# Attention and a quantised feed-forward: the maximum of h over partitions through TensorE, the first group's integers by chunks, gate and p integers further ahead, k_o alone ahead of the branch

## The chip, the cores and the metric

The kernel runs on one core of a Trainium2 chip. Its engines are TensorE (PE; its weight loads are shown as PEld), VectorE (DVE), ScalarE (ACT), GpSimd (POOL) and SyncE (SP, which here only issues DMA transfers). Each engine works through its own list of instructions in order, and semaphores hold an instruction until its inputs are there. The metric is the device time of one execution in microseconds (us). The kernel before takes 1007.1 us, the median of three runs (1004.01 to 1007.13).

## The reference

The input x has 2 x 2048 rows of 512 numbers; there is a context of 2 x 128 rows. Layernorm has no weights here. Cut to what matters:

```python
x = x + xattn(layernorm(x), ctx, Wq, Wkv)       # one head of 512, 128 keys
h = act_qdq(layernorm(x))                       # 16 bits, ONE scale for the whole tensor
up   = act_qdq(h @ dequant4(w_up).T)            # 1536 columns
gate = act_qdq(h @ dequant4(w_gate).T)          # 1536 columns
sig  = round(sigmoid(gate) * 65536) / 65536
p    = act_qdq(gate * sig)
o    = act_qdq(p * up)
out  = x + o @ dequant4(w_down).T
```

`act_qdq` takes the maximum of the absolute values over the whole tensor, divides it by 32767 for a scale, and rounds the tensor to whole multiples of that scale. So each of h, gate, p, up and o needs a maximum over everything before its first integer can be made. The weights are rounded to 4 bits in blocks of 32.

## The kernel before

The 4096 rows are worked in eight groups t of 512 (TG). The 1536 columns of gate and up are twelve chunks f of 128, taken four at a time (k = 0, 1, 2). In the projections the columns lie on the 128 partitions, the rows along the free axis. An integer of 16 bits is not multiplied as such: it is split into parts that TensorE multiplies exactly, a high part (`sa`, the integer over 4096, rounded), the rest, and a combined third part. The weights are split in three as well. One chunk of a projection for one group, called a row of work below, is `project`: eight matmuls into a sum q (four pieces c of the 512 inner numbers, two parts each) and four into a sum e. ScalarE evacuates q, VectorE subtracts e.

The kernel has four stages.

- **Front** (lines 257 to 506). For each group: x is loaded and transposed, scores, softmax (`e`), `turn` transposes the softmax weights (`pe`) and copies them to SBUF (`eT`), `attend` multiplies with the values (`po`) and adds x (`xt`), `normalise` makes h (Square with a sum, then a power -0.5 on GpSimd, then Identity), and `lift` transposes h into the large tile hT by way of PSUM. The work of neighbouring groups is interleaved. For the last group `attend` and `normalise` go tile by tile of 128 rows. `hmax` collects the maxima of h. In between, a generator prepares the weights of gate (`split_weights`, advanced in steps).
- **Gate** (lines 534 to 588). `over_partitions` reduces hmax along the free axis on VectorE and over the partitions on GpSimd; `act_scale` makes the scale s_h and its reciprocal r_h. hi[t] are the integers of group t, made out of hT: those of group 0 in four pieces on VectorE, those of the others alternately by VectorE and ScalarE, all of them ahead of the gate loop in the program. Then hT's space is given up, and the pools `wkb2` (two g4 buffers) and `wprep` take it. `split_integers` makes the parts. For each group and each k four rows of work give a g4 of 1 MB, which goes to DRAM (`gate_d`); `gmax` collects the maxima. The weights of up and down are prepared one step a row.
- **Up** (lines 597 to 788). Groups run from last to first. The work is counted in 24 tiles j of four chunks and 48 halves c of two chunks (c = 2j + h). A half is two rows of work, an evacuation (`u`, L726), a subtraction (L727), and a store to `up_d`. Beside it `next_gelu` turns a loaded gate tile into integers gi and sq with three ScalarE passes over 128 x 2048 (L624 to L626) and loads the tile after the next; there are two gate buffers and three pairs gi, sq. `integers_of_p` makes p (one VectorE product, L661) in one of three tiles `kept_p` and stores it to `p_d`. `bound` forms |u| times p and keeps its largest value per partition (`pumax`); `fetch_best` finds, per partition, the half where that was largest and fetches its u and p rows with two indirect transfers on GpSimd. The last two halves are still at hand. The exact maximum of the rounded products of these three (`most`) goes through a second all-reduce to `top`, and a flag tells whether that maximum is certain; if it is not, a slow general path recomputes it (a branch at L926, not taken in these runs).
- **Output** (lines 794 to 1024). o's integers and parts are made per 128 rows on VectorE and ScalarE, and each of the 32 sets of rows takes 24 matmuls into yq and 12 into ye with the weights wd. ScalarE scales yq by q_o, GpSimd adds x, VectorE adds ye times e_o, and the rows are stored.

The order of instructions on each engine is fixed when the kernel is built, by a planner that goes through the program by priority (earlier lines first) and by a cost model of when inputs are ready. `in_order` forces one instruction behind another on the same engine, without a wait. All loads and stores named above, other than the two first gate loads and the fetches (GpSimd) and one weight load (ScalarE), are issued by SP in one list, where an issue that must wait holds those behind it.

## Time and profile before

| what | us |
|---|---|
| median of three runs | 1007.1 |
| the profiled execution | 1005.54 |
| its span, first to last instruction | 1003.7 |
| PE busy in the span | 942.7 |
| DVE busy | 810.7 |
| ACT busy | 548.3 |
| POOL busy | 89.6 |
| last transposes of h end | 171.96 |
| first gate matmul | 177.02 |
| first up matmul | 455.62 |
| last up matmul ends | 719.95 |
| first output matmul | 734.52 |

Times in the profile count from the span's start. A timeline line gives the start, the duration, the engine, the line of the kernel, the operation, the tiles it writes and reads, and in brackets how long the engine was idle before it and whose work ended that. A row of work takes TensorE 2.72 us at the full granted clock (the q sums of neighbouring rows start at 379.64, 382.36 and 385.08). The granted clock is either full or half in this trace; it is half after an idle stretch, and after the restart at 734.52 it stays half until 739.9.

### The profile page before, as it was taken

To read this page: it belongs to the slowest core of one execution; us is meant where nothing else is said; L and a number is where in the kernel's file an instruction comes from. 1 tells how busy PE (TensorE), PEld (TensorE's weight loads), DVE (VectorE), ACT (ScalarE), POOL (GpSimd) and SP (SyncE) were. 2 spreads that over 40 slices of the span, in tenths; PEclk is the share of its full clock that TensorE was granted. 3 is DMA by queue.
4 is the path that set the end of the run, shared out by engine and by line. 5 is a ranking of instruction groups with operands and counts; after the bars stand their busy time and mean duration, and the time that the engine had idled before them with its cause. 6 is when DMAs were issued, how large, how long until landed. Compare 5 with 4: busy or idle time off the path is not lost. (4 is left out here: it accounts for less than half of the span.)

```text
span 1003.7 us, 11683 instructions
## 1 busy us (share of the span) xinstructions
PE 942.7 (94%) x4321; PEld 762.9 (76%) x4321; DVE 810.7 (81%) x1000; ACT 548.3 (55%) x652; POOL 89.6 (9%) x67
## 2 busy tenths in 40 slices
PE   6997884999999999999999999999779999999998
PEld 5765652788888878887788788888557888888886
DVE  4579874999998989645899789887889999888882
ACT  2277786532333223226998998897454445444331
POOL 0101111000000000000000000000011232222221
PEclk9999896999999999999999999999879999999999
DMA  9177652987886666698899798988885676755611
GB/s 345 32 304 283 220 220 79 401 313 303 330 355 248 265 210 210 224 353 328 306 363 375 258 366 328 378 320 328 288 311 215 206 269 222 250 190 160 245 66 43
DMA packets 103596, 263.72 MB, mean 263 GB/s; under 512 B 6064, under 2 KB 46000, under 8 KB 94832
## 3 DMA queue, kind: packets, MB, share of 16 engines
q1 hardware_dynamic: 102496, 259.02, 69.4%
q0 software_dynamic: 512, 2.88, 0.8%
q10 hardware_dynamic: 528, 1.05, 0.3%
q8 instruction: 34, 0.56, 0.2%
q14 instruction: 26, 0.21, 0.1%
HBM read 136.05 MB, written 126.88 MB: 262 GB/s over the span
## 5 line engine op out<-in xcount | busy, mean ns | idle before, releaser
L528 PE MATMUL q_g<-parts_g,wg 128*128 128x512 f32 x768 | 195.0, 394 | 5.1 <-ACT parts_g L236 5.1
L528 PEld LDWEIGHTS q_g<-parts_g,wg 128*128 128x128 f32 x768 | 143.5, 189 | 35.4 <-ACT parts_g L236 5.8
L579 ACT ACTIVATE g<-q_g 128x512 f32<-128x512 f32 x96 | 57.3, 599 | 169.6 <-PE q_g L528 158.9
L528 PE MATMUL q_u<-parts_u,wu 128*128 128x512 f32 x576 | 142.4, 390 | 0.6 <-ACT u L726 0.6
L528 PEld LDWEIGHTS q_u<-parts_u,wu 128*128 128x128 f32 x576 | 108.1, 188 | 23.3 <-ACT u L726 1.0
L874 PE MATMUL yq<-wd,o_parts 128*128 128x512 f32 x512 | 122.1, 391 | 0.0
L874 PEld LDWEIGHTS yq<-wd,o_parts 128*128 128x128 f32 x512 | 96.9, 189 | 20.3
L532 PE MATMUL e_g<-parts_g,wg 128*128 128x512 f32 x384 | 104.0, 392 | 0.1
L580 DVE CUSTOM_DVE_ANT_0 g<-g,e_g 128x512 f32<-128x512 f32 x96 | 64.4, 681 | 37.2 <-PE e_g L532 37.0
L532 PEld LDWEIGHTS e_g<-parts_g,wg 128*128 128x128 f32 x384 | 72.3, 189 | 15.6 <-DVE parts_g L238 0.5
L889 POOL TENSOR_TENSOR qx<-yqs,x 128x512 f32<-128x512 f32 x32 | 63.7, 1991 | 204.3 <-ACT yqs L887 167.9
L874 PE MATMUL yq<-first_wd,o_parts 128*128 128x512 f32 x256 | 65.5, 399 | 13.2 <-ACT o_parts L863 13.2
L887 ACT ACTIVATE yqs<-yq,q_o 128x512 f32<-128x512 f32 x32 | 22.0, 686 | 101.8 <-PE yq L874 101.8
L532 PE MATMUL e_u<-parts_u,wu 128*128 128x512 f32 x288 | 77.1, 390 | 0.0
L866 DVE SCALAR_TENSOR_TENSOR o_parts<-sa,oi 128x1536 fp32r<-128x1536 int16 (+2 forms) x41 | 62.8, 1548 | 15.6 <-PE ye L882 15.6
L863 ACT CAST o_parts<-sa 128x1536 fp32r<-128x1536 int16 (+2 forms) x41 | 48.6, 1189 | 43.9 <-DVE sa L860 43.9
L670 DVE CUSTOM_DVE_ANT_0 ua<-ua,pi 128x1024 f32<-128x1024 f32 x46 | 55.9, 1220 | 16.9 <-ACT ua L669 16.7
L862 DVE SCALAR_TENSOR_TENSOR o_parts<-sa,oi 128x1536 fp32r<-128x1536 int16 (+2 forms) x41 | 59.5, 1451 | 10.9 <-PE yq L874 8.5
L874 PEld LDWEIGHTS yq<-first_wd,o_parts 128*128 128x128 f32 x256 | 48.9, 192 | 24.4 <-ACT o_parts L863 14.2
L727 DVE TENSOR_TENSOR u<-u,e_u 128x1024 f32<-128x1024 f32 x47 | 56.9, 1216 | 12.0 <-ACT u L726 11.9
L661 DVE SCALAR_TENSOR_TENSOR pi<-gi,k_p,sq 128x2048 int16<-128x2048 int16 x24 | 56.4, 2349 | 9.7 <-ACT sq L626 9.7
L882 PE MATMUL ye<-wd,o_parts 128*128 128x512 f32 x256 | 63.2, 389 | 0.0
(185 smaller groups left out, 1553.7 us busy)
## 6 DMA issues: line engine op xcount, KB each, us to landing
gate_d<-g SPq DMA_DIRECT2D x24, 1024.0 KB, 5.5
up_d<-u SPq DMA_DIRECT2D x48, 512.0 KB, 7.2
gt<-gate_d SPq DMA_DIRECT2D x22, 1024.0 KB, 8.6
u<-up_d SPq DMA_DIRECT2D x21, 1024.0 KB, 6.5
parts_d<-parts_g SPq DMA_DIRECT2D x6, 3072.0 KB, 10.9
parts_u<-parts_d SPq DMA_DIRECT2D x6, 3072.0 KB, 13.4
p_d<-pi SPq DMA_DIRECT2D x24, 512.0 KB, 9.7
p<-p_d SPq DMA_DIRECT2D x84, 128.0 KB, 3.3
```

Source lines behind the costliest of these rows:

```text
L528: nc.tensor.matmul(q, lhsT=w[:, s, c, :], rhs=parts[:, s, c, :], start=(c + s == 0), stop=(c + s == ND))
L532: nc.tensor.matmul(e, lhsT=w[:, 2, c, :], rhs=parts[:, 2, c, :], start=(c == 0), stop=(c == ND - 1))
L579: nc.scalar.activation(g4[:, i, :], q, AF.Copy, scale=1.0 + 1.0 / BASE)
L580: nc.vector.tensor_tensor_reduce(g4[:, i, :], g4[:, i, :], e, 1.0, LOWEST, ALU.subtract, ALU.max, gtop[:, m : m + 1])
L661: nc.vector.scalar_tensor_tensor(pi, gi, k_p, sq, ALU.mult, ALU.mult)
L670: nc.vector.tensor_tensor_reduce(ua, ua, pi, 1.0, 0.0, ALU.mult, ALU.max, pumax[:, c : c + 1])
L727: less = nc.vector.tensor_tensor(u4[:, both, :], u4[:, both, :], e, ALU.subtract)
L862: made.append(nc.vector.scalar_tensor_tensor(parts[1][:, c], sa[:, c], -BASE, oi[:, c], ALU.mult, ALU.add))
L866: return nc.vector.scalar_tensor_tensor(parts[2][:, c], sa[:, c], BASE + 1.0, oi[:, c], ALU.mult, ALU.subtract)
L874: nc.tensor.matmul(q, lhsT=parts[s][:, f, :], rhs=wd[f][:, s, :], start=(f + s == 0), stop=(f + s == NF))
L882: nc.tensor.matmul(e, lhsT=parts[2][:, f, :], rhs=wd[f][:, 2, :], start=(f == 0), stop=(f == NF - 1))
L889: nc.gpsimd.tensor_tensor(qx, qs, x1[:, m % NU, :], ALU.add)
```

## The change

Four things are changed.

1. `over_partitions_by_pe` is a helper made out of what the kernel did for u: a reduction on VectorE, a transpose on TensorE that lays the 128 partial maxima along every partition's free axis, and a reduction of that. It now serves h too, in a PSUM tile of the front's pool, before the front's pools close. The reduction over partitions on GpSimd remains for gate, for `top` and in the branch. In the front, the last group's eT is copied by VectorE.
2. `first_integers` makes group 0's integers and parts by chunks: chunk 0 rounded by VectorE, 1 to 3 by ScalarE, with the casts between them; the third parts come after all others. In the first tile (n = 0) the q sums of the first two chunks come ahead of their e sums. The integers of groups 1 to 7 stand behind the evacuations and subtractions of the first four rows. The two g4 buffers are two pools; the first lies outside hT's space, which is given up after the first tile. The preparation of up's weights begins at n = 1, with two steps a row for that tile.
3. In the up stage `next_gelu` has two more extra places, after halves 19 and 31 (before: after 1 and 13), and `next_p` has two, at halves 17 and 27. The p of a tile stands behind the evacuation of its first half, no longer ahead of the tile. The load of wd chunks 4 to 7 stands ahead of the store of half 43, no longer behind it.
4. `scale_of_o` is cut in two. `factor_of_o` (k_o) stays ahead of the branch; s_o, q_o and e_o are made after it, behind the first set of output rows. The branch now copies its maximum to a_o.

```diff
         return [a[:, i : i + 1] for i in range(len(stats))]
+    def over_partitions_by_pe(pool, tag, shape, stats, name):
+        m = const.tile([P, 1], F32, name=f"m_{name}")
+        nc.vector.tensor_reduce(m, stats, AX.X, ALU.max)
+        rows = pool.tile(shape, F32, tag=tag, name=f"rows_{name}")
+        rows = rows[:, 0, :P] if len(shape) == 3 else rows[:, :P]
+        nc.tensor.transpose(rows, m.to_broadcast([P, P]), ident)
+        a = const.tile([P, 1], F32, name=f"a_{name}")
+        nc.vector.tensor_reduce(a, rows, AX.X, ALU.max)
+        return a
...
                 eT = wk2.tile([P, NJ, P], F32, tag="eT", name=f"eT_{g}")
-                nc.scalar.copy(eT, pe)
+                if g < NG - 1:
+                    nc.scalar.copy(eT, pe)
+                else:
+                    nc.vector.tensor_copy(eT, pe)
                 return eT
...
             lift(NG - 1, hs.pop(NG - 1))
+            a_h = over_partitions_by_pe(ps_o, "o", [P, D], hmax, "h")
...
+            project_q(w, parts, q)
+            project_e(w, parts, e)
+        def project_q(w, parts, q):
             for c in range(ND):
...
                     )
+        def project_e(w, parts, e):
             for c in range(ND):
...
+        def first_integers(pool_a, r_h):
+            n = hi[0]
+            a = pool_a.tile([P, ND, TG], I16, tag="sa", name="sa_g0")
+            parts = homes[0].tile([P, 3, ND, TG], F32R, tag="parts", name="parts_g0")
+            rounded, casts, made = [], [], []
+            for c in range(ND):
+                if c == 0:
+                    made.append(nc.vector.tensor_scalar(n[:, c], hT[:, c, :TG], r_h, QMAX, ALU.mult, ALU.min))
+                else:
+                    rounded.append(nc.scalar.activation(n[:, c], hT[:, c, :TG], AF.Copy, scale=r_h))
+                made.append(nc.vector.tensor_scalar(a[:, c], n[:, c], 1.0 / BASE, None, ALU.mult))
+                casts.append(nc.scalar.copy(parts[:, 0, c], a[:, c]))
+                made.append(
+                    nc.vector.scalar_tensor_tensor(parts[:, 1, c], a[:, c], -BASE, n[:, c], ALU.mult, ALU.add)
+                )
+                if c:
+                    in_order(rounded[c - 1], casts[c - 1])
+            for c in range(ND):
+                made.append(
+                    nc.vector.scalar_tensor_tensor(
+                        parts[:, 2, c], a[:, c], BASE + 1.0, n[:, c], ALU.mult, ALU.subtract
+                    )
+                )
+            in_order(*made)
+            return parts, casts[-1]
+        def integers_of_h(t):
+            if t % 2:
+                return nc.vector.tensor_scalar(hi[t], hT[:, :, ts(t, TG)], r_h, QMAX, ALU.mult, ALU.min)
+            return nc.scalar.activation(hi[t], hT[:, :, ts(t, TG)], AF.Copy, scale=r_h)
         with ExitStack() as c2:
             wg = [load_parts(wg_d, f, "wg") for f in range(NF)]
-            s_h, r_h = act_scale(*over_partitions(hmax, name="h"), "h")
+            s_h, r_h = act_scale(a_h, "h")
...
             wk1 = c2.enter_context(tc.tile_pool(name="wkb1", bufs=1))
-            for c in range(ND):
-                nc.vector.tensor_scalar(hi[0][:, c], hT[:, c, :TG], r_h, QMAX, ALU.mult, ALU.min)
-            first = split_integers(wk1, homes[0], hi[0], [ND, TG], "g0", ND)
+            first, last_cast = first_integers(wk1, r_h)
             table = const.tile([P, 1], F32, name="table")
-            nc.scalar.activation(table, unit, AF.Sigmoid)
-            for t in range(1, NG):
-                if t % 2:
-                    nc.vector.tensor_scalar(hi[t], hT[:, :, ts(t, TG)], r_h, QMAX, ALU.mult, ALU.min)
-                else:
-                    nc.scalar.activation(hi[t], hT[:, :, ts(t, TG)], AF.Copy, scale=r_h)
-            hpool.__exit__(None, None, None)
-            home1 = tc.tile_pool(name="parts1", bufs=1, side="right")
-            homes.append(ctx.enter_context(home1))
-            wk2 = c2.enter_context(tc.tile_pool(name="wkb2", bufs=2))
-            wpp = c2.enter_context(tc.tile_pool(name="wprep", bufs=1))
+            in_order(last_cast, nc.scalar.activation(table, unit, AF.Sigmoid))
+            g4_homes = [c2.enter_context(tc.tile_pool(name="g4_0", bufs=1))]
             ps_m = c2.enter_context(tc.tile_pool(name="ps_m", bufs=3, space=PSUM))
...
-            steps = chain(split_rows(wpp, ps_t, w_up, wu_d, "u"), split_down(wpp, ps_t))
-            groups, wu = {}, []
+            steps, groups, wu = None, {}, []
             for t in range(NG):
...
                     n = t * NK + k
-                    g4 = wk2.tile([P, NQ, TG], F32, tag="g4", name=f"g4_{n}")
+                    g4 = g4_homes[n % 2].tile([P, NQ, TG], F32, tag="g4", name=f"g4_{n}")
+                    sums = [
+                        [ps_m.tile([P, TG], F32, tag=tag, name=f"{tag}_g{NQ * n + i}") for tag in "qe"]
+                        for i in range(2)
+                    ]
+                    if n == 0:
+                        for i in range(2):
+                            project_q(wg[i], parts, sums[i][0])
                     for i in range(NQ):
                         m = NQ * n + i
-                        q = ps_m.tile([P, TG], F32, tag="q", name=f"q_g{m}")
-                        e = ps_m.tile([P, TG], F32, tag="e", name=f"e_g{m}")
-                        project(wg[NQ * k + i], parts, q, e)
-                        nc.scalar.activation(g4[:, i, :], q, AF.Copy, scale=1.0 + 1.0 / BASE)
-                        nc.vector.tensor_tensor_reduce(
+                        if i < 2:
+                            q, e = sums[i]
+                        else:
+                            q, e = (ps_m.tile([P, TG], F32, tag=tag, name=f"{tag}_g{m}") for tag in "qe")
+                        if n == 0 and i < 2:
+                            project_e(wg[i], parts, e)
+                        else:
+                            project(wg[NQ * k + i], parts, q, e)
+                        evacuated = nc.scalar.activation(g4[:, i, :], q, AF.Copy, scale=1.0 + 1.0 / BASE)
+                        subtracted = nc.vector.tensor_tensor_reduce(
                             g4[:, i, :], g4[:, i, :], e, 1.0, LOWEST, ALU.subtract, ALU.max, gtop[:, m : m + 1]
                         )
-                        advance(steps, 1)
+                        if n == 0:
+                            in_order(subtracted, integers_of_h(2 * i + 1))
+                            if i < NQ - 1:
+                                in_order(evacuated, integers_of_h(2 * i + 2))
+                        if n:
+                            advance(steps, 2 if n == 1 else 1)
+                    if n == 0:
+                        hpool.__exit__(None, None, None)
+                        homes.append(ctx.enter_context(tc.tile_pool(name="parts1", bufs=1, side="right")))
+                        g4_homes.append(c2.enter_context(tc.tile_pool(name="g4_1", bufs=1)))
+                        wpp = c2.enter_context(tc.tile_pool(name="wprep", bufs=1))
+                        steps = chain(split_rows(wpp, ps_t, w_up, wu_d, "u"), split_down(wpp, ps_t))
                     abs_max(gmax[:, n : n + 1], g4, AX.XY)
...
-        wd, ready = [], []
+        wd, ready, made_p = [], [], []
...
-        def integers_of_p(j):
+        def next_p():
+            j = len(made_p)
+            if j == len(order):
+                return
             gi, sq = ready[j]
             pi = kept_p[j % NK]
+            made_p.append(pi)
             nc.vector.scalar_tensor_tensor(pi, gi, k_p, sq, ALU.mult, ALU.mult)
...
             )
-            return pi
...
         LAST = len(order) - 1
+        more_gelu = (1, NH // 4 + 1, 3 * NH // 8 + 1, 5 * NH // 8 + 1)
+        more_p = (NH // 3 + 1, NH // 2 + 3)
         for j, (t, k) in enumerate(order):
...
             u4 = tiles_u[j % NK]
-            if j:
-                pi = integers_of_p(j)
             for h in range(2):
...
                         abs_max(umax[:, LAST + 1 + i : LAST + 2 + i], v)
+                if t == 0 and k == 0 and h == 1:
+                    load_down(range(NE, NE + NQ), slice(0, 2))
                 stored = nc.sync.dma_start(out=up_d[c], in_=u4[:, both, :])
-                if h == 0:
+                if h == 0 or c in more_gelu:
                     next_gelu()
-                if c == 0:
-                    pi = integers_of_p(0)
-                if c in (1, NH // 4 + 1):
-                    next_gelu()
+                if h == 0 or c in more_p:
+                    next_p()
+                pi = kept_p[j % NK]
                 if c + 3 < NH:
...
                 abs_max(umax[:, j : j + 1], u4[:, :2, :], AX.XY)
-            if t == 0 and k == 0:
-                load_down(range(NE, NE + NQ), slice(0, 2))
...
-        m_u = const.tile([P, 1], F32, name="m_u")
-        nc.vector.tensor_reduce(m_u, umax, AX.X, ALU.max)
-        rows = ps_m.tile([P, 2, TG], F32, tag="q", name="rows_u")[:, 0, :P]
-        nc.tensor.transpose(rows, m_u.to_broadcast([P, P]), ident)
-        a_u = const.tile([P, 1], F32, name="a_u")
-        nc.vector.tensor_reduce(a_u, rows, AX.X, ALU.max)
+        a_u = over_partitions_by_pe(ps_m, "q", [P, 2, TG], umax, "u")
...
-        def scale_of_o(a_o):
+        def factor_of_o():
...
             nc.vector.reciprocal(k_o, k_o)
+        def scale_of_o():
             nc.vector.tensor_tensor(s_o, a_o, s_pu, ALU.mult)
...
         uis = {0: up_integers(0)}
+        a_o = const.tile([P, 1], F32, name="a_o")
         in_order(rounded[0], *round_up(uis[0], 0, 0, P))
         scale_of_pu()
-        a_o = const.tile([P, 1], F32, name="a_o")
         nc.vector.tensor_reduce(a_o, top[:, 0:3], AX.X, ALU.max)
...
             nc.vector.scalar_tensor_tensor(flag, top[:, 3:4], floor, a_o, ALU.max, ALU.is_le)
-        scale_of_o(a_o)
+        factor_of_o()
         known = nc.values_load(flag[0:1, 0:1], min_val=0, max_val=1)
...
                 a, = over_partitions(omax, name="om")
+                nc.vector.tensor_copy(a_o, a)
                 for k in range(NK):
...
                 scale_of_pu()
-                scale_of_o(a)
+                factor_of_o()
...
                 if m == 0:
+                    scale_of_o()
                     in_order(casts[-1], *round_up(ui, 0, P, P))
...
```

## The prediction

> **What bounds the kernel now.** I read the page's slices first, then the list of waits, then the timelines of the places they name. The slices (each a fortieth of the span, 25 us) show TensorE full in the gate, up and output stages, with two dips, each beside a drop of the granted clock.
>
> ```profile
> PE   6997884999999999999999999999779999999998
> ...
> PEclk9999896999999999999999999999879999999999
> ```
>
> Wherever TensorE is full, work taken off another engine gives nothing; only what shortens the dips, or makes a new one, moves the end. TensorE's waits say what ends the dips:
>
> ```profile
> PE yq L874 <- ACT o_parts L863: 13.2, 3, 12.4
> ...
> PE q_g L528 <- ACT parts_g L236: 5.1, 1, 5.1
> PE po L431 <- ACT eT L419: 4.8, 1, 4.8
> ...
> PE q_u L528 <- ACT u L726: 1.4, 2, 0.9
> ```
>
> The timeline of the first dip (start, duration, in brackets the idle time before and its releaser):
>
> ```profile
> 153.17 0.57 ACT L419 COPY eT<-pe 128x512 f32<-128x512 f32 x1
> ...
> 153.79 5.49 PE L431 MATMUL po<-vsb,eT 128*128 128x512 f32 x6 [4.77 <-ACT eT L419]
> ...
> 169.80 0.17 DVE L140 TENSOR_REDUCE m_h<-hmax 128x1 f32<-128x11 f32 x1
> ...
> 172.00 1.01 ACT L472 COPY hT<-ht 128x1024 f32<-128x1024 f32 x1 [1.15 <-PE ht L471]
> 173.59 0.38 POOL L142 PARTITION_ALL_REDUCE a_h<-m_h  x1 [5.65 <-issue]
> ...
> 174.00 0.15 DVE L151 TENSOR_SCALAR s_h<-a_h 128x1 f32<-128x1 f32 x1 [4.04 <-POOL a_h L142]
> ...
> 177.02 2.10 PE L528 MATMUL q_g<-parts_g,wg 128*128 128x512 f32 x4 [5.06 <-ACT parts_g L236]
> ```
>
> The local maximum is there at 169.97; it comes back from GpSimd only at 173.97. From the scale (r_h, 174.35) to the first gate matmul take 2.67 us more. The second dip:
>
> ```profile
> 720.47 1.08 POOL L685 DMA_INDIRECT best<-up_d,row  x1 [261.86 <-DMA up_d<-u]
> 721.85 0.97 POOL L685 DMA_INDIRECT best<-p_d,row  x1 [0.30 <-issue]
> ...
> 729.62 1.23 DVE L786 CUSTOM_DVE_ANT_0 product_b<-ui_b,best 128x1024 f32<-128x1024 int16 x1 [3.12 <-DMA best<-p_d,row]
> ...
> 733.22 0.48 DVE L859 SCALAR_TENSOR_TENSOR oi<-pi,k_o,ui 128x256 int16<-128x256 int16 x1 [0.82 <-DVEq L926]
> ...
> 734.52 3.78 PE L874 MATMUL yq<-first_wd,o_parts 128*128 128x512 f32 x8 [12.39 <-ACT o_parts L863]
> ```
>
> The last up projection ends at 719.95. What the output stage waits for is the fetched best row (p part landed at 729.6), its product, one all-reduce, the branch. The other two products were done at 726.5.
>
> **The change, part by part.** The sum is made against the profiled execution: 1005.54 us, span 1003.7 and 1.84 around it, 1.56 below the median of 1007.1.
>
> *eT of the last group on VectorE.* On ScalarE it stood behind four Squares of group 6 and started at 153.17, though its transposes ended at about 149.0. VectorE ends the reduction of group 5 and a reciprocal at 150.17 and then idles until 153.31. A copy of this shape by VectorE took 0.66 (kT, L380), so eT is there at 150.8: 3.0 us earlier. Behind it stand the four po products, four residual adds and the per-tile normalisation of group 7. In before, the adds waited behind group 6's reduction (157.88), because VectorE had nothing earlier; with eT at 150.8 all four can precede it. The far end is what ScalarE idles before its last Identity (169.04): 3.9 us in four gaps after 157.85, plus 1.7 before 154.92 (the 0.57 of eT and a wait of 1.18) that group 7's Squares can fill, 5.6. The near end is 0, since group 6's Identity at 154.92 does not wait for eT. I take −3.0, the step's own shift, nearest to the middle.
>
> *Maximum by TensorE, first group by chunks.* The same helper stands in the kernel for u: m_u ends at 721.68, rows_u is 0.29, a_u ends at 722.45, so 0.77 from maximum to maximum against 4.0 now. r_h would come 3.2 earlier, at 171.1. But ScalarE has the last hT copy until 173.01, and it must round chunk 1 and cast chunk 0 (0.57 each, the row of parts_g's cast: 1.14 for 2): first matmul at about 174.25, so −2.8. If the roundings go ahead of that copy, TensorE starts at about 172.5: −4.5. If the transpose queues behind the last eight transposes (to 171.96) it is −2.8 still, as ScalarE is the later of the two. Then three rows of work (36 matmuls) took 10.22 us, 177.02 to 187.24, where 36 take 8.16 at full rate. Half-rate clock until 180.08 explains 1.5; the remaining 0.6 is waiting for parts in between. With single chunks and two q sums open at once, the four chunks arrive in about 4.2 us while 16 matmuls at half rate need 6.9, so that 0.6 goes. Together −3.4; ends −2.0 (the first cast late by one rounding) and −5.1.
>
> *Integers of groups 1 to 7 between the evacuations.* Four of 1.22 on VectorE and three of 2.0 on ScalarE, as now. In the four rows of 10.9 us, ScalarE has 6.0 + 4 × 0.6 and VectorE 6.2 (parts) + 4.9 + 2.8: both fit, three sums of each kind are buffered, and TensorE covers it. Cost 0; without that cover VectorE would be 3 us late. The first g4 now stands outside hT's space, so its evacuation no longer waits (2.76 before 186.59), which TensorE hardly felt. The first w_u load starts about 2 us later behind r_h, and two steps a row catch up: 0, hidden by the buffered rows.
>
> *The library of the all-reduce.* The trace has two pool-configuration instructions at 167.94, right behind the last pow, and the first all-reduce runs at 173.59, 5.65 later; the next two answer in 0.5. Without the h reduction this falls on a_g (m_g ready at 458.14, answer at 458.62). GpSimd is free from 453.99, after the second gate load, so 5.65 ends at 459.64: a_g is 1.4 late. Behind it on ScalarE stand the three one-column activations and the evacuation of u's first half (460.53), needed by TensorE at 466.5, and the first gelu at 463.35, which waits for a transfer. So 0, and +1.4 to +3.6 (load counted from m_g, as 169.97 to 173.59) if that transfer is early.
>
> "GPSIMD Engine Reference" of the Trainium skill, section 2.1, says that the first call to a freshly loaded kernel pays about 6 us with no visible instruction. It speaks against this change, since the price is moved and not removed; the row of 5.65 agrees. Counted in full behind m_g, the 6 us would make a_g 5.5 late and the sum, if all of it reached TensorE, 1002.5; counted from the last GpSimd work, as the row has it, the sum stays at 997.0.
>
> *Gate and p integers further ahead.* The same 24 gelus (2.0 + 2.0 + 1.9) and 24 products of 2.35, but two more gelus are put in at halves 19 and 31 and two p at 17 and 27. Now two extra ones (halves 1 and 13) are followed by stalls:
>
> ```profile
> 484.04 2.11 PE L528 MATMUL q_u<-parts_g,wu 128*128 128x512 f32 x8 [0.88 <-ACT u L726]
> ...
> 561.73 2.11 PE L528 MATMUL q_u<-parts_u,wu 128*128 128x512 f32 x8 [0.56 <-ACT u L726]
> ```
>
> ScalarE is 92.7 of 100 us busy from 500 to 600 and 86.2 from 600 to 700: 21 idle against 11.8 pulled forward. It fits, but an evacuation placed behind two or three activations of 2 us comes late. Two more stalls at 0.7 (561.73 with its slow start): +1.4. Ends −1.0 (the regular gaps close) and +4 (both like 484.04 and 492.15 together, doubled). On SP the gate load that waits for a gelu stands before stores and group loads; group 0's parts were issued at 660.56, take 13.4, and are needed at 687: 13 us of room. VectorE's p products move behind the up evacuation of the same half; bound, their reader, sets nothing there.
>
> *The tail.* ScalarE runs the last gelu at 694.80–701.5, and the evacuations of halves 43 and 44 and their adds (703.88) are late behind it. Half 45's add, with q ready at 708.2, would be at 709.2–710.4 instead of 710.71–711.9; its bound, the maximum and the row at about 714.7 instead of 716.1. Its up store starts 1.5 earlier, and the four wd loads (2 MB, issued at 705.55) go ahead of half 43's store, at about 698. Stores land in 4.0 here by the median, 8.4 in the one that held GpSimd (712.0 to 720.47). So both fetches start at about 715 and land by 722–725. Then the third product follows the second (726.5) at once and ends at 727.6, not 730.85: −3.2, which is the cap. If the store still takes 8.4, −1.5; if DMA stays as full, −0.8.
>
> *k_o alone.* Four scalings (731.82 to 732.40) leave the way to the branch; VectorE's load of the flag stood at 732.2, the others' at 731.8: −0.35, ends 0 and −0.4. They come back behind the first output rows, 0.15 each, covered by TensorE at half clock until 739.9; else +0.6.
>
> Sum: −3.0 − 3.4 + 0 + 1.4 − 3.2 − 0.35 = −8.55: 997.0 us. By the median it would be 998.5. A restart at half rate costs according to where it falls: 3.06 us to full clock after 177.02, 5.34 after 734.52, half of it lost, so about 1 us either way at each dip. I take 997.5.
>
> **The rivals.** *The front swallows it.* ScalarE's own chain (group 6's Identity, hT copies) and not eT sets m_h: 0 for the first term and −2.0 for the second; with the rest 997.0 + 3.0 + 1.4 = 1001.4. For it: 154.92 stays. Against: ScalarE idles 3.9 us behind it, for group 7.
>
> *The up stage gives it back.* Both added gelus, 11.8 us, take most of their length from TensorE, 9 instead of 1.4: 997.0 + 7.6 = 1004.6, no change. For it: the wait of 0.88 behind the first extra. Against: the 21 idle us.
>
> *Slower: SP held.* Gate loads wait for late gelus and hold the groups' loads behind them. From 13 us of hold TensorE waits; three gelus (17.7) make 4.7, and 1.7 of half clock, at three of the group changes: 19.2, 1016. For it: 659.65 to 660.56 already stand in that order. Against: ScalarE is never three gelus behind in the trace.
>
> **How the numbers follow.** Forecast 0.62, front 0.17, given back 0.11, SP 0.10. Three runs of before span 3.1 us, so 0.3% is about what can be told from nothing: faster is below 1004.1. Forecast and front lie there: 0.79; same 0.11; slower 0.10. The forecast's own range is 991 to 1001 (−5.6, −5.1, −1, −3.3 against −1.5, −2.0, +3, −1.5); with the front and most of the given-back case 991 to 1004.5.
>
> **What would show it.** eT on VectorE near 150.8 and the po wait below 2; a_h from DVE and TensorE's q_g wait well below 5; a_g's wait on GpSimd near 2; no gelu behind half 39, and the waits of q_u at ScalarE at most doubled; the best fetches near 715, no wait of product_b for DMA; the wait of yq near 9. I am wrong if m_h does not move, if q_u's waits sum above 5, or if parts_u appears as TensorE's releaser.

## The result and the profile after

The changed kernel took 995.2 us in the median of four executions (991.85 to 997.65), the kernel before 1006.8 beside it: a ratio of 0.989, interval 0.987 to 0.991. The forecast was 997.5. The profiled execution of the changed kernel took 997.23 us, with a span of 995.4; before it was 1005.54 and 1003.7. The two profiles differ by 8.3 us, the medians by 11.6, so the profile shown here is one of the longer executions.

The slices and TensorE's longest waits of the changed kernel answer to those of before:

```profile
PE   6998886999999999999999999999598999999998
...
PEclk9999897999999999999999999999899999999999
```

```profile
PE yq L940 <- ACT o_parts L929: 13.1, 2, 8.9
...
PE q_g L547 <- ACT parts_g L567: 2.6, 1, 2.6
PE q_u L547 <- ACT u L799: 2.3, 2, 1.4
PE po L445 <- DVE eT L433: 1.8, 1, 1.8
```

The wait of po fell from 4.8 to 1.8, of q_g from 5.1 to 2.6, the longest of yq from 12.4 to 8.9. The sum for yq stayed at 13 us, though: it now holds a second long wait, which was not there before. The timeline of the first dip:

```profile
149.04 0.66 DVE L433 COPY eT<-pe 128x512 f32<-128x512 f32 x1
149.75 0.70 PE L445 MATMUL po<-vsb,eT 128*128 128x512 f32 x1 [1.78 <-DVE eT L433]
...
163.79 0.17 DVE L148 TENSOR_REDUCE m_h<-hmax 128x1 f32<-128x11 f32 x1
164.22 0.42 PE L151 MATMUL rows_h<-ident,m_h 128*128 128x128 f32 x1
164.68 0.29 DVE L153 TENSOR_REDUCE a_h<-rows_h 128x1 f32<-128x128 f32 x1 [0.73 <-PE rows_h L151]
165.20 0.16 DVE L164 RECIPROCAL r_h<-s_h 128x1 f32<-128x1 f32 x1
...
167.29 0.80 PE L547 MATMUL q_g<-parts_g,wg 128*128 128x512 f32 x1 [2.64 <-ACT parts_g L567]
```

Per-partition maximum to global maximum is 1.0 us here (163.96 to 164.97), where it was 4.0 through GpSimd. The first gate matmul comes at 167.29 instead of 177.02. The second dip, and the new wait behind it:

```profile
707.91 1.19 POOL L756 DMA_INDIRECT best<-up_d,row  x1 [255.45 <-DVE u L800]
709.39 0.95 POOL L756 DMA_INDIRECT best<-p_d,row  x1 [0.30 <-issue]
...
717.65 1.22 DVE L852 CUSTOM_DVE_ANT_0 product_b<-ui_b,best 128x1024 f32<-128x1024 int16 x1
721.00 0.48 DVE L925 SCALAR_TENSOR_TENSOR oi<-pi,k_o,ui 128x256 int16<-128x256 int16 x1 [0.87 <-ACTq L994]
722.29 3.78 PE L940 MATMUL yq<-first_wd,o_parts 128*128 128x512 f32 x8 [8.92 <-ACT o_parts L929]
...
753.06 3.45 PE L940 MATMUL yq<-first_wd,o_parts 128*128 128x512 f32 x8 [4.15 <-ACT o_parts L929]
```

The last up matmul ends at 711.20 (before: 719.95). From there to the first output matmul, which I call the tail, it is 11.09 us instead of 14.57. The 4.15 at 753.06 stands at the fourth set of output rows. Stage by stage, the changed kernel was ahead by 9.7 us at the first gate matmul, 9.5 at the first up matmul, 8.75 at the end of up, 12.2 at the first output matmul, and 8.3 at the end.

The start of the front differs between the profiles by up to 3 us, for no cause that the runs show: the maxima of group 5 (a reduction of 2.29 us on VectorE, the last step that the change leaves alone) start at 147.80 in before, at 146.75 and 147.16 in the two profiles of the changed kernel, and between 145.52 and 148.50 in the others. Below I count the front from that start and call it G.

### The profile page after: what moved, and what is told of

It is laid out like the page before. It is cut to its first block, busy times and chain, and to the rows that moved or that the text cites. A ratio compares the mean times of both kernels' runs of the same rounds, so it can differ in the third digit from the quotient of the medians.

```text
span 995.4 us, 11700 instructions
## 1 busy us (share of the span) xinstructions
PE 942.0 (95%) x4322; PEld 764.5 (77%) x4322; DVE 804.8 (81%) x999; ACT 547.3 (55%) x654; POOL 87.2 (9%) x66
## 3 DMA queue, kind: packets, MB, share of 16 engines
q10 hardware_dynamic: 528, 1.05, 0.3%
## 5 line engine op out<-in xcount | busy, mean ns | idle before, releaser
L940 PEld LDWEIGHTS yq<-wd,o_parts 128*128 128x128 f32 x512 | 96.7, 189 | 20.3
L553 PEld LDWEIGHTS e_g<-parts_g,wg 128*128 128x128 f32 x384 | 71.9, 188 | 14.9
L955 POOL TENSOR_TENSOR qx<-yqs,x 128x512 f32<-128x512 f32 x32 | 61.6, 1926 | 210.0 <-ACT yqs L953 165.5
L932 DVE SCALAR_TENSOR_TENSOR o_parts<-sa,oi 128x1536 fp32r<-128x1536 int16 (+2 forms) x41 | 58.6, 1448 | 21.4 <-PE ye L948 21.4
L928 DVE SCALAR_TENSOR_TENSOR o_parts<-sa,oi 128x1536 fp32r<-128x1536 int16 (+2 forms) x41 | 59.5, 1451 | 13.8 <-PE yq L940 12.3
L741 DVE CUSTOM_DVE_ANT_0 ua<-ua,pi 128x1024 f32<-128x1024 f32 x46 | 56.0, 1219 | 12.3 <-ACT ua L740 12.2
L553 PEld LDWEIGHTS e_u<-parts_u,wu 128*128 128x128 f32 x288 | 54.0, 188 | 11.3
## 6 DMA issues: line engine op xcount, KB each, us to landing
p_d<-pi SPq DMA_DIRECT2D x24, 512.0 KB, 10.2
```

The source lines that it names most:

```text
L553: nc.tensor.matmul(e, lhsT=w[:, 2, c, :], rhs=parts[:, 2, c, :], start=(c == 0), stop=(c == ND - 1))
L741: nc.vector.tensor_tensor_reduce(ua, ua, pi, 1.0, 0.0, ALU.mult, ALU.max, pumax[:, c : c + 1])
L928: made.append(nc.vector.scalar_tensor_tensor(parts[1][:, c], sa[:, c], -BASE, oi[:, c], ALU.mult, ALU.add))
L932: return nc.vector.scalar_tensor_tensor(parts[2][:, c], sa[:, c], BASE + 1.0, oi[:, c], ALU.mult, ALU.subtract)
L940: nc.tensor.matmul(q, lhsT=parts[s][:, f, :], rhs=wd[f][:, s, :], start=(f + s == 0), stop=(f + s == NF))
L955: nc.gpsimd.tensor_tensor(qx, qs, x1[:, m % NU, :], ALU.add)
```

## The experiments

Each kernel is timed against the kernel before on the same chip. The medians of before in the four sets of runs are 1006.8, 1006.4, 1006.3 and 1006.0. I set times from different sets beside each other to within about 2 us; smaller claims rest on the traces.

### The changed kernel again

Unedited.

> The changed kernel itself again. Theory S: the next group's up tiles land a fixed 40 us after the last up matmul, because SP issues them behind all wd loads, the branch and ten p loads; ScalarE's list has their rounding ahead of the casts of the fourth set of output rows, so TensorE waits about 4 us there in every run. Rival D: that wait of 4.15 is one run's crowded DMA; it is below 1 us in this profile. Both: 991 to 998 us.

Measured: 994.34 us (993.78 to 995.68), ratio 0.988, interval 0.986 to 0.990; span 992.5. The tail is 11.09 again. The wait at the fourth set is 1.72, not 4.15: it is there in this profile too, but neither theory had its size.

### The next group's up tiles ahead of p on SP

```diff
                     one = nc.sync.dma_start(
                         out=pi[:, ds(NQ * k + 2 * h, 2), :], in_=p_d[c, :, :, ts(t % NS, TD)]
                     )
+                    if t in (NS, NS + 1):
+                        in_order(*ups[:NK], one)
```

`ups` holds the three loads of `load_up`.

> The changed kernel with the three loads of the next group's up tiles ahead of the twelve p loads in SP's list (forced order, nothing else). S: they are issued some 7 us earlier, the wait of the fourth set falls from about 4 to below 0.6, and the end comes 3 to 4 us earlier than in the changed kernel. D: the transfers land no earlier, because the engines are full, and the end stays within 1 us.

Measured: 994.4 us (993.15 to 994.56), ratio 0.988, interval 0.986 to 0.990. ScalarE's timelines show what happened. First the changed kernel run again, then this one:

```profile
742.90 0.62 ACT L929 CAST o_parts<-sa 128x512 fp32r<-128x512 int16 x1 [2.33 <-DVE sa L926]
744.98 1.15 ACT L903 ACTIVATE ui<-u,r_u 128x1024 int16<-128x1024 f32 x1 [1.46 <-DMA u<-up_d]
747.58 1.15 ACT L903 ACTIVATE ui<-u,r_u 128x1024 int16<-128x1024 f32 x1 [1.45 <-DMA u<-up_d]
750.05 1.15 ACT L903 ACTIVATE ui<-u,r_u 128x1024 int16<-128x1024 f32 x1 [1.32 <-DMA u<-up_d]
751.10 1.12 ACT L929 CAST o_parts<-sa 128x512 fp32r<-128x512 int16 x2
```

```profile
742.42 0.62 ACT L933 CAST o_parts<-sa 128x512 fp32r<-128x512 int16 x1 [2.14 <-DVE sa L930]
742.94 3.23 ACT L907 ACTIVATE ui<-u,r_u 128x1024 int16<-128x1024 f32 x3
746.74 0.62 ACT L933 CAST o_parts<-sa 128x512 fp32r<-128x512 int16 x1 [0.57 <-DVE sa L930]
```

In the first, ScalarE waits three times for a loaded up tile, and the fourth set's casts stand behind them. In the second SP issues the three loads 19.3 us after the last up matmul instead of 26.4, all three tiles are there, and the casts come 4.4 us earlier (4.0 counted from the last up matmul). TensorE's wait at the fourth set is gone; one of 0.97 appears at 758.57, at the fifth set, for which VectorE works without a gap from 747.43 on and waits for no load: it is the next limit there. From the first output matmul to the end it is 269.1 instead of 269.9. So the mechanism of theory S holds, but not the 3 to 4 us that it expected at the end: the run that I had sized it by was the worst one, and it is worth about 1 us, which the times do not resolve.

The other runs show why this wait is new. The fourth set starts 39.4 to 42.3 us after the last up matmul in every kernel without this edit, whether the tail is long or short: 42.0 in before (tail 14.57, wait 0.21), 41.9 and 40.3 in the two profiles of the changed kernel (tail 11.09, waits 4.15 and 1.72). What the tail gains beyond that point is lost again, because SP reaches these loads only behind its other loads and the branch: it issued them 26.1 to 29.0 us after the last up matmul, 28.5 in before and 29.0 in the profiled changed kernel. That also gives the size of the wait. SP's last loads of wd each stand until an earlier one has landed; the last of them left 14.9 us after the last up matmul in the profiled changed kernel and 12.2 in its second profile, the up tiles' loads at 29.0 and 26.4, and the waits are 4.15 and 1.72. With the loads ahead the fourth set starts at 38.1.

### Gelus and p at their old places

```diff
-                if h == 0 or c in more_gelu:
+                if h == 0 or c in (1, NH // 4 + 1):
                     next_gelu()
-                if h == 0 or c in more_p:
+                if c == 0:
                     next_p()
```

and for the later tiles `next_p` ahead of the tile.

> The changed kernel with gelus and p at their old places (extra gelus after halves 1 and 13 only, p of a tile ahead of its first half); the wd load ahead of half 43's store stays. The first output matmul comes about 14.2 us after the last up matmul, not 11.1, and the up stage is up to 0.8 us shorter. S: the 3.1 us are not seen at the end, because the wait of the fourth set takes them up: within 1 us of the changed kernel. Rival, that the tail's gain reaches the end: 2.3 to 3.2 us slower.

Measured: 993.76 us (990.51 to 995.30), ratio 0.987, interval 0.984 to 0.989. The tail stays at 11.11, not 14.2 as expected. The gelus ahead are not what shortens it, at least not alone.

What the new places do cost is read from TensorE's waits in the up stage. All eight profiles with the new places have a wait for ScalarE's evacuation of 0.9 to 2.1 us between 672 and 678; none of the six with the old places has one there. ScalarE then works through four gelus with hardly a gap (646 to 677 in the profiled changed kernel), the last of them 0.44 us late because its gate tile lands at about 669, and an evacuation stands behind its first pass. The load of the last group's parts is also late. First the profiled changed kernel, with two of TensorE's rows, then SP in before:

```profile
661.21 0.34 SPq L678 DMA_DIRECT2D gt<-gate_d  x1
...
662.14 0.36 SPq L673 DMA_DIRECT2D parts_u<-parts_d  x1
...
672.04 2.14 PE L547 MATMUL q_u<-parts_u,wu 128*128 128x512 f32 x8 [1.44 <-ACT u L799]
...
678.29 2.29 PE L547 MATMUL q_u<-parts_u,wu 128*128 128x512 f32 x9 [0.47 <-DMA parts_u<-parts_d]
```

```profile
660.56 0.38 SPq L605 DMA_DIRECT2D parts_u<-parts_d  x1
```

In the changed kernel SP issues this load 18.9 us after the first matmul of the next to last group (643.23), because it stands behind a gate load that waits for a gelu; in before it is 6.2 us (after 654.36). With the new places it is 18.9 to 19.2 in all eight profiles, with the old ones 6.2 to 7.9 in all six. The room of 13 us that the prediction counted on is used up: the parts land at 678.15, when TensorE has already run out of work.

### The maximum of h by GpSimd

```diff
-            a_h = over_partitions_by_pe(ps_o, "o", [P, D], hmax, "h")
+            a_h, = over_partitions(hmax, name="h")
```

> The changed kernel with the maximum of h over partitions by GpSimd as before; eT, chunks and all else as changed. From m_h to r_h about 4.4 us, not 1.4; a_g answers in about 0.5 us, not in 3.8. If the library's 6 to 8 us are hidden behind gate's last rows and the up stage's first sums: 3.0 us slower than the changed kernel. If a late a_g costs the up stage what the front gains: within 1 us.

Measured: 997.31 us (996.97 to 998.33), ratio 0.991, interval 0.989 to 0.993: 3.0 above the changed kernel, as expected where the library's wait is hidden. From the start of m_h to the start of r_h it takes 4.11 us, against 1.09 to 1.41 in the profiles with the helper and all else as changed. a_g, in turn, answers 0.5 us after m_g, as in before; in the ten profiles with the helper it starts 3.7 to 6.4 us after m_g. The 2.7 to 3.0 us that the helper gains ahead of r_h all arrive in the time, so the late a_g costs little.

### eT back on ScalarE

```diff
-                if g < NG - 1:
-                    nc.scalar.copy(eT, pe)
-                else:
-                    nc.vector.tensor_copy(eT, pe)
+                nc.scalar.copy(eT, pe)
```

> The changed kernel with the last group's eT back on ScalarE. Theory E (eT on VectorE frees the whole of ScalarE's gap, so group 7's Squares run in it): the maximum of h is ready about 5 us later than in the changed kernel (169 to 170 instead of 164 to 165), and the time is 4 to 5 us above the changed kernel's 994.3, so 998 to 999.5. Theory F (only eT's own shift counts, as my prediction took it): 3 us later, 997.3. Theory G (ScalarE's own chain sets the maximum): no difference, 994.3.

Measured: 1000.66 us (998.39 to 1003.24), ratio 0.994, interval 0.992 to 0.997. The timeline:

```profile
153.87 0.58 ACT L430 COPY eT<-pe 128x512 f32<-128x512 f32 x1
...
170.51 0.16 DVE L148 TENSOR_REDUCE m_h<-hmax 128x1 f32<-128x11 f32 x1
...
174.53 2.07 PE L544 MATMUL q_g<-parts_g,wg 128*128 128x512 f32 x4 [1.62 <-ACT parts_g L564]
```

m_h starts 22.0 after G (170.51 − 148.50), exactly as in before (169.80 − 147.80). In the profiled changed kernel it is 17.0 (163.79 − 146.75), in the second profile 18.0. So eT alone is worth 4 to 5 us at the maximum of h, 4.9 to 5.5 at the first gate matmul (26.0 after G, against 20.5 and 21.2), and about 6 in the times, 1 to 2 more than theory E had; where the rest comes from is not shown. Theory E's mechanism stands; 3.0 was too little, and the rival in which ScalarE's own chain sets the maximum is out.

### The load of wd back behind half 43, and the third part undone

```diff
-                if t == 0 and k == 0 and h == 1:
-                    load_down(range(NE, NE + NQ), slice(0, 2))
                 stored = nc.sync.dma_start(out=up_d[c], in_=u4[:, both, :])
...
+            if t == 0 and k == 0:
+                load_down(range(NE, NE + NQ), slice(0, 2))
```

> The changed kernel with the load of wd chunks 4 to 7 back behind the store of half 43; the gelus and p products stay ahead. Theory W (what matters is when SP gets to this load, and the gelus ahead alone bring half 43's store and so the load forward by some 11 us): the load still issues near 695, the last up stores find the DMA engines free, the fetch starts within 2 us of the last row number, and from the last up matmul to the first output matmul it stays 11.1 us: the time is 994.3, within 1 us. Theory P (the load's place in the list is what made the tail short): 14.5 us from the one to the other, 997.7.

Measured: 995.6 us (992.85 to 998.66), ratio 0.989, interval 0.987 to 0.992; tail 11.09. For the tail theory W is right and P is out; the 1.3 us above the changed kernel are not resolved by the times. Then the same with the gelus and p at their old places too:

> The changed kernel with the gelus and p products at their old places and the load of wd chunks 4 to 7 back behind the store of half 43: the whole third part undone. Theory W: SP stands at half 43's store until about 704, the 2 MB of the load fill the DMA engines from 704 to 716, the first fetch starts 8 us late, and the tail is 14.2 us instead of 11.1 (14.57 before, less 0.35 for k_o alone): +3.1, less up to 0.8 that the gelus ahead cost in the up stage, so 996.6 to 997.4. If the tail stays at 11.1, the old tail was the chance of one run of the kernel before, or belongs to another part: 994.

Measured: 993.76 us (992.07 to 995.16), ratio 0.987, interval 0.985 to 0.990; tail 11.10. With nothing of the third part left, the tail stays short: theory W was wrong in saying that the third part makes it. Its first half, that the place of the load in time decides, is still open here. ScalarE's lists say more. First before, then this kernel, around the last gelu:

```profile
694.80 1.99 ACT L624 ACTIVATE gi<-gt,r_g 128x2048 int16<-128x2048 f32 x1
696.82 2.01 ACT L625 ACTIVATE gt<-gi,s_g 128x2048 f32<-128x2048 int16 x1
698.74 1.04 ACT L669 ACTIVATE ua<-u 128x1024 f32<-128x1024 f32 x1
699.69 1.90 ACT L626 ACTIVATE sq<-gt 128x2048 uint16<-128x2048 f32 x1
701.49 2.15 ACT L726 ACTIVATE u<-q_u 128x1024 f32<-128x1024 f32 x2
```

```profile
685.41 1.99 ACT L692 ACTIVATE gi<-gt,r_g 128x2048 int16<-128x2048 f32 x1
687.78 1.03 ACT L801 ACTIVATE u<-q_u 128x1024 f32<-128x1024 f32 x1 [0.38 <-PE q_u L547]
688.70 2.00 ACT L693 ACTIVATE gt<-gi,s_g 128x2048 f32<-128x2048 int16 x1
```

The evacuation of half 43 (L726, L801) stands behind the whole gelu in before, and behind its first pass here. So half 43's store and the load behind it leave early without the third part. The planner has ordered ScalarE differently, with the code of this stage in effect as before. So another part of the change has to be behind it. The next two runs try the maximum of h, and the order by itself; eT, the chunks and k_o were not undone beside the third part in any run.

### Both undone, and the order alone

```diff
-            a_h = over_partitions_by_pe(ps_o, "o", [P, D], hmax, "h")
+            a_h, = over_partitions(hmax, name="h")
```

on top of the kernel with the third part undone.

> The changed kernel with the third part undone and the maximum of h taken by GpSimd again. With the third part undone alone the tail had stayed at 11.1 us, and ScalarE's list had the evacuation of half 43 ahead of the last gelu's second pass, where the kernel before has it behind the third. In this kernel's list it is behind the third again. Theory L (the tail is set by where that evacuation stands, since half 43's store and the 2 MB load of wd stand behind it in SP's list): the load issues some 14 to 15 us ahead of the end of the last up matmul, the fetch starts about 8 us late, the tail is 14.2 us (14.57 less 0.35 for k_o), and the time is 993.8 + 3.0 (the maximum) + 3.1 = 999.9. Theory D (a crowded transfer in one run of the kernel before): the tail stays at 11.1 us and the time is 996.8.

Measured: 999.93 us (998.35 to 1000.39), ratio 0.994, interval 0.992 to 0.995. The tail is 14.20 (713.90 to 728.10). SP and GpSimd in this kernel, and then with the third part undone alone:

```profile
699.49 2.13 SPq L770 DMA_DIRECT2D wd<-wd_d  x4
702.36 3.87 SPq L814 DMA_DIRECT2D up_d<-u  x2
...
714.17 1.07 POOL L756 DMA_INDIRECT best<-up_d,row  x1 [263.27 <-DMA p_d<-pi]
```

```profile
690.51 2.18 SPq L770 DMA_DIRECT2D wd<-wd_d  x4
...
707.09 1.19 POOL L756 DMA_INDIRECT best<-up_d,row  x1 [252.33 <-DVE u L802]
```

The old order is back, with the old tail: theory L stands and D is out. Against the end of up (713.90 and 710.41) the load leaves 14.4 and 19.9 us ahead, the fetch 0.3 after and 3.3 before. The windows of the same two kernels (PE, PEld, DVE, ACT, POOL busy, then clock, DMA share, GB/s) show what the load meets:

```profile
704.00:708.00 4.00, 4.00 (x19) 3.34 (x18) 3.96 (x4) 1.47 (x2) 0.00 (x0) 1.00 1.02 344
708.00:712.00 4.00, 4.00 (x20) 3.30 (x19) 3.85 (x10) 1.22 (x2) 0.00 (x0) 1.00 1.03 413
```

```profile
704.00:708.00 4.00, 4.00 (x20) 3.30 (x19) 3.86 (x8) 1.63 (x2) 0.91 (x1) 1.00 0.42 164
```

Counted from the end of up, the second line of the first kernel and the line of the second are the same stretch, with DMA shares of 1.03 and 0.42. Late, the load fills the DMA engines while the last halves are stored; early, they are half free just when the stores that the fetch waits for leave. A smaller part, 0.8 us, is that VectorE has the row numbers earlier (the maximum they come from starts 5.3 instead of 4.5 us ahead of the end of up). The order alone, in the kernel before (`evacuated` is the evacuation of the half, `second` holds the gelus' second passes):

```diff
-                if h == 0:
+                if h == 0 and c + 6 != NH:
+                    next_gelu()
+                if c + 5 == NH:
                     next_gelu()
+                    in_order(evacuated, second[-1])
```

> The kernel before with nothing changed but the place of the last gelu: it is put behind half 43's evacuation and subtraction in the program, and its second pass is ordered behind that evacuation on ScalarE. Theory L: half 43's store leaves about 12 us earlier, the load of wd with it, and from the last up matmul to the first output matmul it takes 11.4 us instead of 14.57: 3.1 below the kernel before, 1003.2, ratio 0.997. Theory D: the tail stays as it is and so does the time, ratio 1.000.

Measured: 1004.61 us (1003.51 to 1008.34, twelve executions), ratio 0.9987, interval 0.9974 to 0.9999. The tail is 11.36 (723.67 to 735.03), 3.2 shorter, as theory L has it. Counted from the end of up, half 43's store leaves 20.3 us ahead instead of 14.8: 5.5 earlier and not 12, and that is enough. The time gained 1.4 instead of 3.1. In the profile the wait at the fourth set of output rows is 2.57, where before has 0.21: most of the difference comes back there, as in the changed kernel. The profiled execution is the longest of the twelve (span 1006.6), so no sum is made on it.

### Without the chunks

```diff
-            first, last_cast = first_integers(wk1, r_h)
+            for c in range(ND):
+                nc.vector.tensor_scalar(hi[0][:, c], hT[:, c, :TG], r_h, QMAX, ALU.mult, ALU.min)
+            first = split_integers(wk1, homes[0], hi[0], [ND, TG], "g0", ND)
```

> The changed kernel with group 0's integers and parts as in the kernel before: four pieces rounded by VectorE, then the parts by the general helper; the order of the q sums and the places of the other integers stay. Theory J (the chunks are worth the 0.7 us between r_h and the first matmul, and the 0.6 of waits inside the first rows, half of it hidden by the half clock): 0.7 to 1.4 us above the changed kernel's 994.3, so 995 to 995.8. Theory H (half clock swallows them): no difference. Theory K (the chunks bring most of what the second part brings): 2.5 us or more.

Measured: 995.7 us (994.72 to 997.02), ratio 0.990, interval 0.988 to 0.992. From r_h to the first gate matmul it takes 2.84 us, as in before (2.83), against 2.1 with chunks: 0.74. The trace shows theory J's first term. The time, 1.4 above 994.34 from another set of runs, is too small a difference to tell J from H; K, with 2.5 or more, fits neither.

### TensorE kept busy while it waits

```diff
+            def keep_busy(after, pool, tag, shape, times, name):
+                spare = pool.tile(shape, F32, tag=tag, name=f"spare_{name}")
+                spare = spare[:, 0, :] if len(shape) == 3 else spare
+                in_order(after, *[nc.tensor.transpose(spare[:, ts(i % 4, P)], ident, ident) for i in range(times)])
```

called at three places.

> The changed kernel with transposes of the identity into spare PSUM tiles while TensorE would be idle: 12 between the last two lifts, 16 behind the maximum of h, 44 behind the maximum of u. They compute nothing that is used. Theory C (the half clock after a restart comes from the idle stretch before it): the granted clock is full from the first gate matmul on and soon after the first output matmul, where now it is half for 3.6 to 6.7 us and for 3.9 us; half of that is lost, so 1.8 to 3.3 and up to 1.9 us are won: 990 to 992.5. Theory N (the half clock follows the time or the load on TensorE, not idleness): it is half all the same, 994.3; if the transposes themselves run at half clock they can hold the first matmuls up by 1 to 3 us.

Measured: 997.76 us (996.59 to 1001.92), ratio 0.993, interval 0.990 to 0.995: slower than the changed kernel. At the gate theory C holds: the first 16 matmuls take 3.98 us, where they took 6.67 and 5.52 in the two profiles of the changed kernel, and theory N is out there. But the transposes between the lifts (2.01 us) hold up the last eight of h, and r_h stands 20.3 after G instead of 18.4 and 19.1. At the output it fails: the 44 transposes end at 720.95, TensorE then idles 4.12 us, and the first eight matmuls take 3.78 as without them. The up stage was 269.0 long instead of 265.1 and 265.7, with waits of q_u on ScalarE of 1.23, 1.51 and 2.08. The first two follow on a first gelu that starts 10.7 us after the first up matmul (8.3 and 9.5 in the changed kernel's profiles), the third is the one near 672 that all kernels with the new places have, and 3.4 us at half clock come after it. The run of the wd load at its old place has the same pattern (first gelu at 10.2, waits of 0.70, 1.51 and 1.99, 3.4 us at half clock) and 268.3, so the transposes are not needed for it; why the first gelu is late there is not shown.

### What the runs point to, put together

The changed kernel with the third part undone, the up tiles' loads ahead, and 16 transposes behind the maximum of h only.

```diff
+            spare = ps_o.tile([P, D], F32, tag="o", name="spare")
+            in_order(by_pe[0], *[nc.tensor.transpose(spare[:, ts(i % 4, P)], ident, ident) for i in range(16)])
```

> A version put together from the runs: the changed kernel with the third part undone (the up stage took 262.6 us with it undone, 265.7 with it), the three loads of the next group's up tiles ahead of the p loads on SP, and 16 transposes of the identity on TensorE behind the maximum of h, none elsewhere. From the profile with the third part undone (991.7): 1.5 less for the clock after the first gate matmul (16 matmuls in 4.0 us instead of 5.5) and 1.8 less for the wait in the output stage (2.8 down to 1.0): span 988.4, time about 990.5. Rival: the waits move elsewhere, as the run with more transposes showed: 994.

Measured: 989.39 us (988.56 to 990.12), ratio 0.983, interval 0.981 to 0.985. No execution of it is as long as the shortest of the other versions. At the gate:

```profile
163.28 2.13 PE L525 MATMUL spare<-ident 128*128 128x128 f32 x16
166.13 4.08 PE L551 MATMUL q_g<-parts_g,wg 128*128 128x512 f32 x16 [0.72 <-ACT parts_g L571]
```

The windows from the first gate matmul to the fourth row, here, in the profiled changed kernel, and in before:

```profile
166.13:174.59 8.46, 8.46 (x36) 6.76 (x37) 7.63 (x15) 8.32 (x10) 0.00 (x0) 1.00 1.01 417
```

```profile
167.29:178.33 11.04, 11.04 (x37) 8.89 (x37) 7.63 (x15) 9.19 (x12) 0.00 (x0) 0.73 1.01 420
```

```profile
177.02:187.24 10.22, 10.16 (x36) 7.29 (x37) 10.15 (x17) 7.43 (x9) 0.00 (x0) 0.86 1.03 414
```

The granted clock is 1.00 here, 0.73 and 0.86 there. Three rows cost 8.46 us instead of 11.04 and 10.22. In the ten profiles of kernels with the same first matmuls and no transposes behind the maximum of h, these 16 took 5.50 to 6.67 us; in the two with transposes they took 3.98 and 4.08. There is no wait at the fourth output set; one of 0.67 stands at the fifth, so the rival, that all the waits move elsewhere, is out.

## Why the prediction was right, point by point

The total held: −8.55 forecast against the profiled execution, −8.3 measured. That it came so close is in part luck. The 8.3 are made up of 1.05 from the start of the front, which the change does not explain, 4.96 for eT, 3.7 up to the first gate matmul for the maximum and the chunks, and 3.48 in the tail, less 0.2 in the gate stage, 0.8 in the up stage and 3.9 in the output stage, for which the sum had no term. The upper end of the stated range, 1001, does not follow from the terms listed for it: they sum to −2.0, which gives 1003.5. The result lies inside either.

**eT on VectorE: forecast −3.0, measured −4 to −5.** The step that I took, "the step's own shift, nearest to the middle", was too near. Once eT is early, all four adds precede group 6's reduction (in before only the first did), and two of group 7's Squares run on ScalarE ahead of group 6's Identity, which is where the far end of the working (−5.6) had looked. m_h came 4.96 earlier counted from G, and putting eT back cost 6 us of time.

**Maximum and chunks: forecast −3.4, measured about −3.** The maximum is worth 3.0 (997.31 against 994.34). The chunks give 0.74 to the first matmul. The row of the same helper (0.77 for u) was a good price. The wait inside the first rows did go, but the half clock lasted longer: until 5.9 us after the first gate matmul against 2.9 in before. That took it back, with 11.04 for three rows against 10.22; in the second profile 3.4 us at half clock gave 9.89.

**The library: forecast 0, and so it was, with a different size.** I had 5.65 from the end of GpSimd's last work, so a_g 1.4 late. In the profiled execution it was 8.10 (7.7 to 9.5 in the ten profiles with the helper), and a_g came 3.4 later behind m_g than in before. So the wait was moved and not removed. "GPSIMD Engine Reference" of the Trainium skill, section 2.1, gives about 6 us for the first call of a freshly loaded kernel: the 5.6 to 5.8 with h's reduction on GpSimd agree, the 8.10 is longer, and the measurement decides. What hid it was the first gelu: its gate tile landed at 452.08 and a_g was there at 452.46. From first up matmul to first gelu it is 8.3 us, before 7.7. In the second profile a_g came 1.4 us behind the tile, the gelu started at 9.5, and TensorE's first wait for an evacuation was 1.49 instead of 0.85, so some 0.6 us of the price may show there.

**Gelus and p ahead: forecast +1.4, measured 0.9 to 2.1 as waits.** The size was about right, the place was not: I had priced two more stalls at the added gelus, and one came, near 672, where the gelus ahead run into one another. The length of the stage does not resolve it. With the new places it was 264.3 to 269.0 us in eight profiles, 265.8 on average; with the old ones 262.6 to 266.7 in six, 264.5 on average, and 264.3 in before. The cause of much of that spread is another one: the later the first gelu starts after the first up matmul (7.4 to 10.7 us), the longer TensorE waits soon after (0.6 to 3.1 us), in kernels of both kinds. parts_u did appear as TensorE's releaser, with 0.47, which I had named as a sign of being wrong, and rightly so: it belongs to the rival in which SP is held.

**The tail: forecast −3.2 and −0.35, measured −3.48, but from another cause.** The chain was read rightly: a late evacuation of half 43, a 2 MB load behind its store, a fetch that waits. The step that failed is the attribution: "ScalarE runs the last gelu at 694.80–701.5, and the evacuations of halves 43 and 44 and their adds (703.88) are late behind it", to be cured by the third part. Either the third part or the helper for the maximum cures it, the latter because the planner then puts this evacuation ahead of the gelu's second pass, 520 us further on (why it does is not shown; I take it to be the other times in its cost model). Only with both undone is the tail 14.2 again. I had taken ScalarE's order of before as given wherever the diff does not touch it. k_o alone has no run of its own; the tail of 14.20 with both undone, against 14.57, and the 11.09 to 11.11 of the kernels with a short tail against 11.36 with the order alone, leave about 0.25 to 0.37 for it.

**Not in the sum: 1.5 to 4 us in the output stage.** I costed everything up to the first output matmul and let the rest stand. The fourth set waits for up tiles whose time does not depend on the tail, so with a tail 3.5 shorter this wait grew from 0.2 to between 1.5 and 4.15. In the profiled execution this offset the surplus of eT and the early start of the front.

**The rivals.** "The front swallows it" fell with the place of m_h after G, 17.0 against 22.0. "The up stage gives it back" was right in kind and much smaller than the 9 us that it needed. "SP held" did occur, but stayed just short of its price: the load of group 0's parts was held 12.7 us longer than in before, the rival needed more than 13, and TensorE waited 0.47 us in the profiled execution and not at all for it in the other seven profiles with the new places.

## What to carry to other kernels

A gain ends at the next thing whose time does not move with it: after costing a dip, list what the engines behind it wait for, and whether those loads move too. Where a planner orders the engines, a small edit can reorder a stage far from it, so compare the engines' lists, not only the diff, before a gain is put down to a part. A copy that stands behind other work on a busy engine is worth the gaps that it lets others fill, not only its own shift.

## What was not expected of the hardware

- The first all-reduce of GpSimd after other GpSimd work started 5.6 to 5.8 us after GpSimd was free at the end of the front, and 7.7 to 9.5 at the start of the up stage, where the helper makes the reduction of gate the first of the program. In these ten profiles it starts between 0.5 us before and 1.2 us after the landing of the gate load that GpSimd had issued just ahead of it (452.09 against 452.08 in the profiled changed kernel). Whether that transfer is what makes it longer was not tried.
- After the wait of 2.64 us ahead of the gate, the granted clock over the next three rows was 0.73 in one execution and 0.83 in another of the same kernel; with transposes filling the wait up to 0.72 us it was 1.00. Ahead of the output stage, transposes that ended 4.12 us before the restart gave nothing: the clock went to half 2.2 us after the last of them. So the filling has to reach nearer to the restart; how near was not tried.
- The half clock comes in steps: in the fourteen traces every stretch of it but the last, at the program's end, lasts 3.41 us or two to five times that. The first gate matmul fell 0.15 us before a step of 3.41 in one profile of the changed kernel, and 7.7 us into a stretch of 13.65 in the other.
- The same 36 matmuls of the first three gate rows took 8.46, 9.89 or 11.04 us, nearly all of it by this clock (8.46 at full clock, 3.4 and 5.9 us at half clock in the others), two of these in the same kernel: an edit near a restart cannot be priced to better than 1 us from one profile.
